# Sturm sweeps of an in-kernel eigensolver: each recurrence step as one double-width product and one sum

## The chip, the cores and the metric

The kernel runs on one core of a Trainium2 chip. The metric is the device time of one execution in microseconds. The kernel before took 2164.6 us (median of three runs, 2164.06 to 2165.33).

## The reference

Four graph layers act one after the other on `x` of 128 graphs with 64 nodes and 256 features in float32; all graphs share one 64x64 matrix `adj`. Each layer is `x = x + layer(relu(layernorm(x)), adj, weights)`.

```
layer 0:  two graph convolutions relu(adj @ (h W + b)), then four small LSTMs
          over windows of 1, 2, 3 and 4 nodes, each writing its last state back
layer 1:  h <- relu(layernorm(L_norm h Wc + bc)) + h with L_norm = 2 adj / lam_max - I
          masked 4-head attention, gelu MLP, layernorms
layer 2:  graph attention (leaky scores, masked softmax)
layer 3:  _, U = eigh(D^-1/2 (deg - adj) D^-1/2)
          out = U relu(U^T h W1 + b1) W2 + ...
```

What matters here is layer 3: it needs all 64 eigenvectors `U` of one 64x64 symmetric matrix. The kernel computes them on the chip itself. The matrix is brought to tridiagonal form with diagonal `D` and off-diagonal `E`. Eigenvalues are then found by multisection: for a trial value x, the number of sign changes in the Sturm sequence

```
p[0] = 1,   p[1] = (d[0] - x) p[0],   p[k+1] = (d[k] - x) p[k] - e[k-1]^2 p[k-1]
```

tells how many eigenvalues lie below x. Every sweep narrows the interval of every eigenvalue to an eighth.

## The kernel before, in words

**Main work.** The 8192 rows of `x` are 64 tiles of 128 rows. Layer 0 works through eight groups of eight tiles: layer norm, two mixing products, the LSTMs, and a transposition back; the results go to DRAM (`put`). The 16 groups of four tiles that follow (the stage called REST in the code, groups from `REST` up) run layers 1, 2 and 3 with their x resident in SBUF, and write the output.

**The eigensolver** (`eig_decomp`, lines 347 to 885, called in line 1107) is a separate group, `EIG` (line 1094), of small instructions on 64 partitions, most of them on VectorE. All its tiles are parts of one large SBUF tile named `arena`, so in a profile everything of it is found under that name until the arena is given to REST. In order of time it does a Householder reduction (62 steps), the set-up of three nested tridiagonal problems (index `l`), nine Sturm sweeps (`NSWEEP`, line 634), a forward and backward quotient recurrence (line 681), eigenvectors, and a correction; lines 1108 to 1113 write the block-diagonal tiles `Ub` and `UTb` that layer 3 needs. The normalising factor for `lapb`, the mixing matrix of layer 1, comes from its own chain of matrix squarings and does not depend on the eigensolver.

**One sweep** (lines 635 to 663). Each of the 64 partitions holds one eigenvalue index. There are C = 21 columns: three problems times KS = 7 trial values. `DX[k]` = d[k] - x is made by six instructions of 448 elements. Then comes the recurrence over k (lines 643 to 653), in which `PL[k]` holds p[k]: a product `DX[k] * PL[k]`, from k = 1 on a product `b = PL[k-1] * E2[k-1]`, and a difference, each 21 elements wide. After every eighth step two neighbouring rows of PL are rescaled by four more instructions. The sweep ends with the signs (`SG`, 1365 elements), the sign changes (`NE`, 1344 elements, written over DX), their count (a reduction over k), a comparison, a sum, and the new lower bounds `lo`, on which the next sweep depends. So the sweeps are one long chain of dependent instructions.

**The order of the work** is neither written by hand nor left to the engines: every instruction is recorded in a `Plan`, which simulates all five engines with a cost for each instruction (lines 176 to 220: for a VectorE instruction on n elements mostly 0.075 + 0.00105 n us, and 0.12 us more until a dependent instruction may begin), and writes the resulting order into each engine's queue. The queues are worked off in that order. `EIG` is the group set aside (line 328): its VectorE and GpSimd instructions have the lowest rank, and are put in only where nothing else is ready; its matmuls have the highest. In the plan, GpSimd and VectorE instructions on SBUF alone also exclude each other. The `arena` counts as a set of spare buffers for REST from the moment at which the last instruction of `EIG` is done (line 963).

Of the kernel before, what the change touches and what calls it, by code (L numbers as in the profile page):

```python
# [8 lines left out]
ALU = mybir.AluOpType  # L9
# [3 lines left out]
N = 64  # L13
KS = 7
# [332 lines left out]
def eig_decomp(plan, room, adj, adjT, ident, idf, ones):  # L347
# [13 lines left out]
    V, G, PE, ACT, SP = (plan.proxy(e) for e in ("V", "G", "PE", "ACT", "SP"))  # L361
# [3 lines left out]
    def scope():  # L365
        inner.reset([0])
        return inner

    def T(shape, name):
        return room.tile(shape)  # L370

    def W(shape, name, bufs=None):

        if bufs is None:
            bufs = 2 if shape[-1] < N or name == "lab" else 1
        ring = kept.setdefault((name, tuple(shape)), [])
        if len(ring) < bufs:
            ring.append(room.tile(shape))
        else:
            ring.append(ring.pop(0))  # L380
        return ring[-1]
# [56 lines left out]
    ph = scope()  # L438
# [4 lines left out]
    for k in range(N - 2):  # L443
# [17 lines left out]
        s = W([N, 1], 's')  # L461
# [21 lines left out]
        p = pf[:N, :2 * N]  # L483
# [43 lines left out]
    M = N - 1  # L527
# [68 lines left out]
    E2 = T([N, 3, N], 'E2')  # L596
# [30 lines left out]
    V.tensor_copy(lo, l1.to_broadcast([N, 3]))  # L627
    C = 3 * KS
    ph = scope()
    PL = ph.tile([N, N + 1, C])  # L630
    V.memset(PL[:, 0, :], 1.0)
    DX = ph.tile([N, N, 3, KS])
    SG = ph.tile([N, N + 1, C])
    for s_ in range(NSWEEP):
        V.tensor_scalar(w, w, 1.0 / (KS + 1), None, op0=ALU.mult)
        x = W([N, 3, KS], 'x')
        V.tensor_scalar(x, c['ramp'], w, None, op0=ALU.mult)
        V.tensor_add(x, x, lo.unsqueeze(2).to_broadcast([N, 3, KS]))
        for l in range(3):
            V.tensor_mul(DX[:, :, l, :], BM[:, l, :].unsqueeze(2).to_broadcast([N, N, KS]), x[:, l, :].unsqueeze(1).to_broadcast([N, N, KS]))  # L640
            V.tensor_sub(DX[:, :, l, :], DM[:, l, :].unsqueeze(2).to_broadcast([N, N, KS]), DX[:, :, l, :])
        DXf = DX.rearrange('p k l s -> p k (l s)')
        for k in range(N):
            V.tensor_mul(PL[:, k + 1, :], DXf[:, k, :], PL[:, k, :])
            if k:
                b = W([N, 3, KS], 'b', 2)
                V.tensor_mul(b, PL[:, k - 1, :].rearrange('p (l s) -> p l s', l=3), E2[:, :, k - 1:k].to_broadcast([N, 3, KS]))
                V.tensor_sub(PL[:, k + 1, :], PL[:, k + 1, :], b.rearrange('p l s -> p (l s)'))
            if k % 8 == 7 and k < N - 1:
                mm = W([N, C], 'mm')  # L650
                V.tensor_reduce(mm, PL[:, k:k + 2, :].rearrange('p k c -> p c k'), op=ALU.max, axis=AX.X, apply_absolute_value=True)
                V.tensor_scalar(mm, mm, 1e-30, None, op0=ALU.max)
                V.reciprocal(mm, mm)
                V.tensor_mul(PL[:, k:k + 2, :], PL[:, k:k + 2, :], mm.unsqueeze(1).to_broadcast([N, 2, C]))
        V.tensor_scalar(SG, PL, 0.0, None, op0=ALU.is_lt)
        NE = DXf
        V.tensor_tensor(NE, SG[:, 1:, :], SG[:, :N, :], op=ALU.not_equal)
        ct = W([N, 3, KS], 'ct')
        V.tensor_reduce(ct.rearrange('p l s -> p (l s)'), NE.rearrange('p k c -> p c k'), op=ALU.add, axis=AX.X)
        V.tensor_tensor(ct, ct, li.unsqueeze(2).to_broadcast([N, 3, KS]), op=ALU.is_le)  # L660
        sm = W([N, 3], 'sm')
        V.reduce_sum(sm, ct, axis=AX.X)
        V.scalar_tensor_tensor(lo, sm, w, lo, op0=ALU.mult, op1=ALU.add)
# [7 lines left out]
    ph = scope()  # L671
# [80 lines left out]
    def one(name):  # L752
        return W([N, 1], name)
# [7 lines left out]
    for l in (1, 0):  # L761
# [10 lines left out]
        b = one('bc')  # L772
# [11 lines left out]
        t = W([N, N], 't64')  # L784
# [3 lines left out]
        t = W([N, N], 't64')  # L788
# [23 lines left out]
        t = W([N, N], 't64')  # L812
# [120 lines left out]
def gnn_kernel(ctx: ExitStack, tc: tile.TileContext, a, out):  # L933
# [171 lines left out]
    room = Carver(arena)  # L1105

    QT, Vc, inner = eig_decomp(plan, room, adj2[:N], adjT2[:N], ident[:N, :N], ident, ones)
    for dst, lhs, rhs in ((Ublk, QT, Vc), (UTblk, Vc, QT)):
        l2 = inner.tile([P, 2, N])
# [564 lines left out]
```

## Time and profile before

| Item | Value |
|---|---|
| median of three runs | 2164.6 us (2164.06 to 2165.33) |
| the profiled execution's own time | 2165.9 us |
| its span, first to last instruction | 2164.1 us |
| outside its span | 1.8 us |
| VectorE busy, instructions | 1800.3 us (83%), 7402 |
| GpSimd busy, instructions | 653.1 us (30%), 968 |
| granted TensorE clock | 0.996 of full speed |

In the profile PE is TensorE's matmuls, PEld its weight loads, DVE is VectorE, ACT ScalarE, POOL GpSimd, SP the DMA-issuing SyncE. Since every instruction is issued by one helper, all have the same line number, L344; groups are told apart by tile and shape. A shape such as 64x21 is partitions times elements. [...]two instructions may overlap in the profile, and a busy VectorE can still take in more work.

### The profile page before, as it was taken

Reading aid. Unit: us, or ns where it says so; the run is one execution under the profiler, and the core shown is the slowest. Engines: PE = TensorE matmul, PEld = TensorE weight load, DVE = VectorE, ACT = ScalarE, POOL = GpSimd, SP = SyncE. Lnnn points to the kernel's source line nnn. Section 1 sums busy time; section 2 is a strip of 40 time slices with the busy share of each in tenths; the row PEclk is TensorE's granted clock in tenths of the full one; section 3 lists DMA queues with packets and bytes.
Section 4 is the critical chain, followed back from the end, with each engine's and each line's share of the span. In section 5 each row is a group of like instructions: output and inputs, shape, how many; then the busy total and the mean of one; then the engine's idle time right before and its main releaser. Section 6 shows DMA issues by size and latency. Waiting matters only on the chain.

```text
span 2164.1 us, 45598 instructions
## 1 busy us (share of the span) xinstructions
PE 2112.6 (98%) x16580; PEld 1630.7 (75%) x16580; DVE 1800.3 (83%) x7402; ACT 1079.8 (50%) x2331; POOL 653.1 (30%) x968
## 2 busy tenths in 40 slices
PE   8999999999999999999999999999999999999997
PEld 6688688688678678678778688766777767776776
DVE  5888788889899999899989887568878868885797
ACT  3354354354354354345345345456566655645673
POOL 7221211210200110110110113654456745554353
PEclk9999999999999999999999999999999999999999
DMA  5000100100100100100000213000010000000001
GB/s 205 2 3 22 41 3 22 40 1 21 40 1 20 40 1 20 40 1 21 26 1 23 69 40 97 21 1 2 21 41 21 21 22 21 12 11 11 1 2 60
DMA packets 44866, 57.67 MB, mean 27 GB/s; under 512 B 8928, under 2 KB 38496, under 8 KB 44640
## 3 DMA queue, kind: packets, MB, share of 16 engines
q1 hardware_dynamic: 43536, 53.71, 7.6%
q8 instruction: 130, 2.13, 0.4%
q10 hardware_dynamic: 1104, 1.05, 0.2%
q14 instruction: 96, 0.79, 0.1%
HBM read 37.53 MB, written 16.78 MB: 25 GB/s over the span
## 4 chain that ended last, share of the span: by engine, by line
PE 83%; DVE 11%; POOL 2%; ACT 1%; DMA 1%; issue 1%; SPq 0%; DVEq 0%; ACTq 0%
PE bank L344 83%; DVE arena L344 3%; DVE big L344 3%; DVE stat L344 2%; DVE mids L344 1%; DVE sums L344 1%; POOL stat L344 1%; POOL sums L344 1%; DMA Wih<-in_WihT_dram 1%; ACT mids L344 0%; ACT arena L344 0%; DMA Whh<-in_L_b_dram 0%; DMA big<-put 0%; ACT big L344 0%; SPq L344 0%
## 5 line engine op out<-in xcount | busy, mean ns | idle before, releaser
L344 PE MATMUL bank<-big,Wih 128*128 128x256 f32 (+3 forms) x2400 | 748.2, 435 | 18.7 <-DVE arena L344 9.3
L344 PEld LDWEIGHTS bank<-big,Wih 128*128 128x128 f32 x2400 | 439.9, 190 | 205.0 <-issue 114.4
L344 ACT ACTIVATE mids<-bank,bl 128x256 f32<-128x256 f32 (+3 forms) x528 | 275.4, 528 | 407.3 <-PE bank L344 403.5
L344 PE MATMUL bank<-big,Whh 128*128 128x256 f32 (+2 forms) x1624 | 431.0, 368 | 3.5 <-DVE big L344 3.5
L344 DVE TENSOR_TENSOR arena<-arena 64x21 f32<-64x21 f32 (+5 forms) x2255 | 372.9, 196 | 35.8 <-POOL arena L344 8.2
L344 PEld LDWEIGHTS bank<-big,Whh 128*128 128x128 f32 x1624 | 294.3, 190 | 42.5 <-issue 10.1
L344 PE MATMUL bank<-big,sums 128*128 128x168 f32 (+2 forms) x1728 | 268.8, 307 | 0.0
L344 PEld LDWEIGHTS bank<-big,sums 128*128 128x128 f32 (+1 forms) x1728 | 225.4, 178 | 16.0 <-issue 3.9
L344 POOL TENSOR_SCALAR stat<-stat 128x4 f32<-128x4 f32 (+1 forms) x228 | 67.9, 299 | 485.4 <-DVE stat L344 472.5
L344 ACT COPY mids<-bank 128x168 f32<-128x168 f32 (+2 forms) x393 | 132.1, 357 | 138.1 <-PE bank L344 135.1
L344 DVE TENSOR_TENSOR big<-mids 128x512 f32<-128x512 f32 (+2 forms) x256 | 142.8, 565 | 31.3 <-ACT mids L344 28.6
L344 ACT ACTIVATE mids<-mids,bl 128x336 f32<-128x336 f32 (+2 forms) x192 | 102.4, 540 | 71.4 <-DVE mids L344 67.6
L344 DVE TENSOR_TENSOR mids<-bank,mids 128x168 f32<-128x168 f32 (+2 forms) x307 | 112.9, 372 | 25.8 <-PE bank L344 22.3
L344 DVE SCALAR_TENSOR_TENSOR arena<-arena 64x1 f32<-64x1 f32 (+15 forms) x565 | 120.9, 237 | 7.5 <-POOL arena L344 3.9
L344 POOL TENSOR_TENSOR big<-big 128x168 f32<-128x168 f32 (+1 forms) x24 | 16.8, 712 | 359.9 <-DVE arena L344 132.2
L344 POOL TENSOR_TENSOR stat<-stat,mhalf 128x4 f32<-128x4 f32 (+1 forms) x114 | 122.1, 1072 | 5.7
L344 ACT ACTIVATE mids<-big 128x256 f32<-128x256 f32 (+2 forms) x176 | 89.4, 509 | 67.7 <-DVE big L344 48.8
L344 PE MATMUL bank<-Wih,big 128*128 128x256 f32 (+1 forms) x512 | 111.7, 358 | 0.2 <-ACT big L344 0.2
L344 DVE TENSOR_SCALAR arena<-arena 64x1 f32<-64x1 f32 (+9 forms) x537 | 104.8, 202 | 8.4 <-POOL arena L344 0.8
L344 DVE TENSOR_TENSOR big<-big,mids 128x256 f32<-128x256 f32 (+2 forms) x200 | 99.3, 498 | 11.1 <-ACT mids L344 10.2
L344 PEld LDWEIGHTS bank<-Wih,big 128*128 128x128 f32 x512 | 87.7, 190 | 15.4 <-issue 4.5
L344 ACT COPY big<-bank 128x512 f32<-128x512 f32 x108 | 59.9, 587 | 55.9 <-PE bank L344 50.8
(357 smaller groups left out, 3568.0 us busy)
## 6 DMA issues: line engine op xcount, KB each, us to landing
big<-in_x_dram SPq DMA_DIRECT2D x30, 512.0 KB, 5.2
put<-big SPq DMA_DIRECT2D x16, 512.0 KB, 3.0
Wih<-in_WihT_dram SPq DMA_DIRECT2D x3, 1024.0 KB, 11.8
Whh<-in_WhhT_dram SPq DMA_DIRECT2D x3, 1024.0 KB, 13.8
big<-put SPq DMA_DIRECT2D x6, 512.0 KB, 5.8
arena<-put SPq DMA_DIRECT2D x6, 512.0 KB, 6.6
out_dram<-big SPq DMA_DIRECT2D x12, 256.0 KB, 2.3
out_dram<-arena SPq DMA_DIRECT2D x12, 256.0 KB, 2.3
```

The source lines that it names most:

```text
L344: getattr(self.engines[op.eng], name)(*map(real, args), **{k: real(a) for k, a in kw.items()})
```

## The change

The two factors of a step lie side by side in one new tile `CO[k]`: columns 0 to 20 hold -e[k-1]^2 (written once, ahead of the sweeps, by three instructions of 441 elements), columns 21 to 41 hold d[k] - x (DX is now a view of this half). One product of 42 elements, `PL[k-1:k+1] * CO[k]`, makes both terms, and one addition of its halves makes `PL[k+1]`. The step k = 0 stays a single product. The signs are written over PL instead of into SG, which goes; therefore row 0 of PL has to be set to 1 again in each sweep, which GpSimd does, where VectorE did it once before. The sign changes are written into the DX half of CO, so that their rows lie 42 elements apart instead of 21, as do those of DX.

```diff
     PL = ph.tile([N, N + 1, C])
-    V.memset(PL[:, 0, :], 1.0)
-    DX = ph.tile([N, N, 3, KS])
-    SG = ph.tile([N, N + 1, C])
+    CO = ph.tile([N, N, 2, C])
+    l3 = lambda t: t.rearrange('p k (l s) -> p k l s', l=3)
+    DX = l3(CO[:, :, 1, :])
+    for l in range(3):
+        V.tensor_scalar(l3(CO[:, 1:, 0, :])[:, :, l, :], E2[:, l, :M].unsqueeze(2).to_broadcast([N, M, KS]), -1.0, None, op0=ALU.mult)
     for s_ in range(NSWEEP):
...
-        DXf = DX.rearrange('p k l s -> p k (l s)')
-        for k in range(N):
-            V.tensor_mul(PL[:, k + 1, :], DXf[:, k, :], PL[:, k, :])
-            if k:
-                b = W([N, 3, KS], 'b', 2)
-                V.tensor_mul(b, PL[:, k - 1, :].rearrange('p (l s) -> p l s', l=3), E2[:, :, k - 1:k].to_broadcast([N, 3, KS]))
-                V.tensor_sub(PL[:, k + 1, :], PL[:, k + 1, :], b.rearrange('p l s -> p (l s)'))
+        G.memset(PL[:, 0, :], 1.0)
+        V.tensor_mul(PL[:, 1, :], CO[:, 0, 1, :], PL[:, 0, :])
+        for k in range(1, N):
+            b = W([N, 2, C], 'b', 2)
+            V.tensor_mul(b, PL[:, k - 1:k + 1, :], CO[:, k])
+            V.tensor_add(PL[:, k + 1, :], b[:, 0, :], b[:, 1, :])
...
-        V.tensor_scalar(SG, PL, 0.0, None, op0=ALU.is_lt)
-        NE = DXf
-        V.tensor_tensor(NE, SG[:, 1:, :], SG[:, :N, :], op=ALU.not_equal)
+        V.tensor_scalar(PL, PL, 0.0, None, op0=ALU.is_lt)
+        NE = CO[:, :, 1, :]
+        V.tensor_tensor(NE, PL[:, 1:, :], PL[:, :N, :], op=ALU.not_equal)
```

## The prediction, made before the changed kernel ran

> **What bounds the kernel now.** I read the busy times first, then a table by stage, then the same table for the tile `arena`, then VectorE in order of time, and last the place where the eigensolver hands over.
>
> ```profile
> PE 2112.6 (98%) x16580; PEld 1630.7 (75%) x16580; DVE 1800.3 (83%) x7402; ACT 1079.8 (50%) x2331; POOL 653.1 (30%) x968
> ```
>
> TensorE is busy for 2112.6 of 2164.1 us and the change leaves its work as it is, so no more than the 51.5 us in which it is idle can be won. The stages show where they lie (columns: window, length, busy PE, PEld, DVE, ACT, POOL):
>
> ```profile
> 598.20:1162.10 563.90, 557.06 (x3271) 441.60 (x3270) 519.30 (x2390) 254.81 (x578) 55.25 (x80) 1.00 0.05 16
> 1162.10:1220.00 57.90, 57.90 (x268) 48.49 (x268) 51.61 (x254) 23.54 (x52) 0.00 (x0) 1.00 0.08 24
> 1220.00:1338.00 118.00, 109.32 (x543) 89.92 (x543) 98.00 (x432) 52.14 (x121) 21.12 (x34) 0.99 0.29 93
> 1338.00:1362.00 24.00, 24.00 (x114) 21.13 (x113) 14.08 (x49) 16.68 (x37) 20.25 (x26) 1.00 0.00 1
> 1362.00:2164.00 802.00, 777.65 (x8564) 576.72 (x8563) 621.83 (x1703) 464.59 (x807) 412.56 (x553) 1.00 0.06 18
> ```
>
> The first window holds eight of the nine sweeps: TensorE is idle for 563.90 - 557.06 = 6.8 us in it. In the third the eigensolver's rest runs beside the last group of layer 0, and 8.7 us are idle. REST has 24.4 us. The sweeps thus lie under a full TensorE. For the `arena` alone, the window of the sweeps reads:
>
> ```profile
> 598.20:1162.10 563.90, 0.00 (x0) 0.00 (x0) 339.66 (x1863) 0.00 (x0) 0.00 (x0) 1.00 0.05 16
> ```
>
> So 2390 - 1863 = 527 VectorE instructions of layer 0 are strewn among 1863 of the sweeps. The sign-change instructions (1344 elements) mark the first and the ninth sweep:
>
> ```profile
> 598.16 1.55 DVE L344 TENSOR_TENSOR arena<-arena 64x1344 f32<-64x1344 f32 x1
> ```
>
> ```profile
> 1162.11 1.54 DVE L344 TENSOR_TENSOR arena<-arena 64x1344 f32<-64x1344 f32 x1
> ```
>
> That is 563.95 / 8 = 70.5 us a sweep. VectorE in order of time (start, length, engine, operation, count) shows what a step is made of:
>
> ```profile
> 655.02 0.26 DVE L344 TENSOR_TENSOR arena<-arena 64x21 f32<-64x21 f32 x2
> ...
> 656.54 0.38 DVE L344 TENSOR_TENSOR arena<-arena 64x21 f32<-64x21 f32 x2
> ...
> 658.45 1.61 DVE L344 TENSOR_TENSOR arena<-arena 64x21 f32<-64x21 f32 x11
> ...
> 663.27 0.40 DVE L344 TENSOR_TENSOR arena<-arena 64x42 f32<-64x42 f32 x2
> ```
>
> One such instruction lasts some 0.17 us. Two in 0.26 us start 0.09 apart: the second does not need the first. Two in 0.38 us start 0.21 apart: a dependent pair (the last steps ahead of a rescaling). Eleven in 1.61 us are ten distances in 1.44, or 0.43 for three. So a step of three is no sum of three durations: it is two dependent passages, product to difference and difference to next product, 2 x 0.21 = 0.42 us, and `b`, which needs nothing new, lies in the shadow of the first. The 42-wide rescaling product and its 21-wide successor start 0.40 - 0.17 = 0.23 apart.
>
> [...]177 and 197:
>
> ```profile
> L344 DVE TENSOR_TENSOR arena<-arena 64x21 f32<-64x21 f32 x1728 | 239.8, 177 | 16.1
> ...
> L344 DVE TENSOR_TENSOR arena<-arena 64x42 f32<-64x42 f32 x63 | 12.4, 197 | 1.7
> ```
>
> Doubling the width costs 0.02 us. [...]removing the instruction in the shadow does not shorten a chain. [...]
>
> **The change part by part.**
>
> *The steps.* Nine sweeps x 63 steps = 567. Removed: 567 instructions, all from the shadow. Left are two dependent passages, 0.23 from the wide product to the sum and 0.21 from the sum to the next product: 0.44 us against 0.42, so 567 x 0.02 = 11 us more if nothing comes between. What is won is room: of a step's 0.42 us, three starts of about 0.09 to 0.10 take 0.29 and 0.13 stand empty; afterwards 0.09 + 0.11 = 0.20 of 0.44 are taken and 0.24 stand empty, in two gaps. Layer 0's instructions may lie in those gaps. How well do they today? A sweep alone is 63 x 0.42 = 26.5, seven rescalings of about 1.0 (0.19 + 0.17 + 0.28 + 0.20 with waits), six products and differences of 0.64 less 0.03 overlap = 3.7, signs 0.8, changes 1.5, count 3.1, small ones 1: 43.6 us. 563.9 - 8 x 43.6 = 215 us for 527 instructions, 0.41 each; their busy time is (519.30 - 339.66) / 527 = 0.34. So the gaps are hardly used. With 527 x 9/8 = 593 in all sweeps, the new gap of 0.11 could save at most 62 us (567 x 0.11), at least nothing. Many come in rows, of which only the first finds a gap, and one that arrives late in a gap pushes the chain: I take 10 us. Net of both: +1 us.
>
> *Count of the changes.* 9 x 3.07 us at twice the distance: [...]at worst twice as long, +27.6. I take 0. Signs in place and strided writes in runs of 7 or 21: 0, the same element counts.
>
> *New once:* three instructions of 441 elements, between 0.3 (as fast as the signs per element) and 0.64 (the 448-wide product): 1.7 us. VectorE's single memset goes: -0.1.
>
> *GpSimd's memset,* nine times: it waits for the sign changes of the sweep before and the first product waits for it. Between lie the count (3.07), the comparison, the bounds and six 448-wide instructions (3.7), over 7 us, while GpSimd is busy for 55 of 564 us. If that cover failed, all of VectorE's queue, layer 0 included, would stand behind that product, and TensorE's banks behind it. 0 taken; it is bounded by 9 x 0.5, half the row of a 128x512 memset pair of 1.00 us. No DMA is added or moved.
>
> *Sum:* the eigensolver ends +1 + 1.7 - 0.1 = about 3 us later, bounds -60 (62 saved, 2 added) and +45 (11 + 2 + 27.6 + 4.5). What does that move? The last write of the eigensolver, the first use of an arena buffer by REST on ScalarE as it ends, and TensorE's first read of one:
>
> ```profile
> 1337.87 0.23 DVE L344 COPY UTb<-bank 64x64 f32<-64x64 f32 x1
> ```
>
> ```profile
> 1343.96 1.58 ACT L344 ACTIVATE arena<-big,stat 128x256 f32<-128x256 f32 x3
> ```
>
> ```profile
> 1365.63 3.71 PE L344 MATMUL bank<-lapb,arena 64*64 64x64 f32 x236
> ```
>
> ScalarE has filled them at 1345.5; TensorE works at layer 0 until 1362 and reads them at 1365.6. So an earlier end wins nothing there, and a later one is covered for 20 us. Three microseconds move nothing: **no change**, 2164.6 by the median. The profiled execution took 2165.9 = 2164.1 span + 1.8 around it, 1.3 above the median, and I apply the difference of nothing to the median; I say 2164.0 since more free slots on VectorE can only help layer 0's own instructions a little.
>
> The costs in the plan follow the same picture (0.097 + 0.11 for a 21-wide passage), so it will write an order with nearly the same end of the eigensolver. But every choice from the first sweep on can fall otherwise, and in REST 24.4 us of stalls hang on such choices: a scatter of a few us either way that no row lets me compute.
>
> **The rivals.**
> *Faster, the room is used.* If layer 0's instructions fill the gaps, the sweeps end up to 60 us earlier, the rest of the eigensolver moves from the last group of layer 0 to where TensorE is full anyway, and the 8.7 us of stalls of that stage mostly go: 2164 - 7 = 2157. For it: 527 instructions find 0.24 us per step. Against it: they fill little today.
> *Slower, the end comes too late.* The strided count doubles (+27.6) and the gaps stay empty (+11 + 2): 41 us. Beyond 20 us TensorE meets REST buffers that are not filled. 41 - 20 = 21 us, half of them covered by blocks in other buffers: +10, 2174. It decides from a delay of 20 us.[...]
> *The change doesn't do what it says* cannot be: the counts follow from the loop.
>
> **How the numbers follow.** About 0.2%, 4.3 us, is what can be told from no change here. No change 0.38 (2160.3 to 2168.9 as its own range, 2164.0 predicted), faster 0.34, slower 0.28; the scatter of the order gives the two sides more than their mechanisms would alone. Range 2153 to 2175: from the faster case with 4 us of scatter to the slower one with 1.
>
> **What would show it.** 64x21 products and sums 1728 - 1134 = 594, 64x42 ones 63 + 567 = 630, VectorE 7402 - 565 = 6837 instructions, GpSimd 977. Two dependent instructions in a step at 0.23 and 0.21: if nearer than that, my chain is wrong. Sweeps 70 us apart: at 65 or less the room is used. The count at 3.07 us. `UTb` written at 1341: before 1310 or after 1358 one of the rivals holds. It would be wrong altogether if TensorE's stalls in the sweeps (6.8 us) changed by more than 3.

## The result, and the profile after

| | Before | After |
|---|---|---|
| median, runs side by side | 2164.76 us (2163.33 to 2165.35, 6 runs) | 2172.11 us (2170.70 to 2174.17, 6 runs) |
| profiled execution, its span | 2165.9 us, 2164.1 us | 2172.2 us, 2170.4 us |
| mean granted TensorE clock in it | 0.996 | 0.992 |

The ratio is 1.0030, with a 95% interval of 1.0020 to 1.0041. The change makes the kernel slower by 0.3%, 7.3 us.

Busy time and instructions of each engine, of the changed kernel:

```profile
PE 2120.1 (98%) x16580; PEld 1635.6 (75%) x16580; DVE 1765.8 (81%) x6837; ACT 1075.4 (50%) x2329; POOL 656.1 (30%) x977
```

VectorE has 565 instructions fewer and GpSimd 9 more, as foretold. But look at TensorE. It executes the same 16580 matmuls and is busy for 7.5 us longer (2112.6 before), while its idle time has hardly changed: 2170.4 - 2120.1 = 50.3 us against 51.5. So in this execution the loss is not time in which TensorE waits; the same work takes longer.

The table by stage of the changed kernel, with the same windows as before (window, length, busy PE, PEld, DVE, ACT, POOL, then the granted clock):

```profile
598.20:1162.10 563.90, 556.95 (x3274) 442.04 (x3273) 499.70 (x1890) 254.24 (x581) 57.37 (x88) 0.99 0.06 18
1162.10:1220.00 57.90, 57.90 (x264) 48.02 (x263) 51.60 (x244) 22.63 (x51) 0.00 (x0) 1.00 0.04 15
1220.00:1338.00 118.00, 109.38 (x540) 89.54 (x539) 97.43 (x444) 52.67 (x125) 19.86 (x34) 0.99 0.27 76
1338.00:1362.00 24.00, 24.00 (x113) 21.12 (x112) 12.44 (x47) 16.24 (x37) 21.11 (x26) 1.00 0.16 59
1362.00:2164.00 802.00, 781.21 (x8562) 579.14 (x8561) 610.83 (x1701) 461.92 (x806) 414.16 (x553) 0.99 0.05 17
```

TensorE is idle for 6.95 us in the window of the sweeps (6.84 before) and for 8.6 in the third (8.7 before). One pair of matmuls, which every kernel here executes once, marks on TensorE where REST begins. The tables by tile give its first and last start, before and after:

```profile
L344 PE MATMUL bank<-UTb,ones x2: 272/274/275, 1362.7 to 1362.8; 128*128 128x128 f32 x2
```

```profile
L344 PE MATMUL bank<-UTb,ones x2: 273/274/275, 1363.3 to 1363.4; 128*128 128x128 f32 x2
```

Up to there only 0.6 us is lost. From there to the end of the span it takes 2164.1 - 1362.7 = 801.4 us before and 2170.4 - 1363.3 = 807.1 after. So nearly the whole loss, 5.7 us of 6.3, arises in REST, where no instruction was changed; TensorE is even busier in the window after 1362, 781.21 us of 802 against 777.65.

The eigensolver's last write and a row of seven instructions of the recurrence, VectorE of the changed kernel in order of time:

```profile
643.26 1.50 DVE L344 TENSOR_TENSOR arena<-arena 64x42 f32<-64x42 f32 x7
```

```profile
1336.92 0.23 DVE L344 COPY UTb<-bank 64x64 f32<-64x64 f32 x1
```

Seven instructions in 1.50 us, the last one of 0.17, make six distances in 1.33: 0.222 each, 0.44 for a step of two. `UTb` is written at 1336.92, 1 us earlier than before.

Where does TensorE become slower? A stretch of REST in the changed kernel, TensorE in order of time (start, length, engine, operation, count, and in brackets the idle time ahead of it and who ended it):

```profile
1677.14 3.62 PE L344 MATMUL bank<-Wih,big 128*128 128x256 f32 x16
...
1683.06 2.05 PE L344 MATMUL bank<-Wih,mids 128*128 128x128 f32 x16 [0.58 <-ACT mids L344]
1687.61 0.69 PE L344 MATMUL bank<-UTb,Whh 64*64 64x64 f32 x32 [2.50 <-DVE Whh L344]
1688.23 1.12 PE L344 MATMUL bank<-ident,big 128*128 128x128 f32 x7
1690.64 3.78 PE L344 MATMUL bank<-Wih,big 128*128 128x256 f32 x8 [1.29 <-DVE big L344]
```

At 1677, 16 matmuls of 128x256 take 3.62 us. At 1690, after waits of 0.58, 2.50 and 1.29 us, 8 of the same kind take 3.78: half the speed. The same 50 us in the changed kernel and in the one before:

```profile
1650.00:1700.00 50.00, 45.62 (x563) 37.09 (x563) 44.97 (x142) 25.81 (x48) 29.18 (x47) 0.93 0.14 44
```

```profile
1650.00:1700.00 50.00, 49.14 (x582) 38.44 (x581) 46.34 (x132) 28.54 (x50) 31.56 (x40) 1.00 0.15 44
```

The clock was 0.93 against 1.00, and 4.4 us were idle against 0.9. In the trace's record of the granted clock the stretches at half speed sum to 20.2 us before (6.8 at the start, then 3.4 at 897, 3.4 at 1238, 3.4 at 2125 and 3.1 at the end) and to 36.3 after (10.2 at the start, 6.8 at 894, 3.4 at 1238, 6.8 at 1689, 3.4 at 2129, 3.4 at 2163 and 2.2 at the end). 16.1 us more at half speed are 8 us lost, about the 7.5 us by which TensorE is busier. 9.3 of the 16.1 us, 4.7 us lost, lie in REST (6.8 at 1689, and 9.0 against 6.5 near the end).

This execution overstates the clock's part somewhat: its mean granted clock of 0.992 is the lowest of the six runs of the changed kernel, whose mean is 0.9937. The three sets of runs of the kernel before that stand beside the experiments have 0.9959 to 0.9965 on average. At half speed half of the time is lost, so the loss is 1 minus the clock, times the span: 13.7 us against 7.5 to 8.8. By this estimate 5 to 6 of the 7.3 us are the clock's.

What lies ahead of the 6.8 us at half speed? They begin at 1689.0, behind the waits of 0.58 and 2.50 us and ahead of the one of 1.29; in the 3.41 us before, half as long as the stretch itself, TensorE was still busy for 1.34 us (window, length, busy PE, PEld, DVE, ACT, POOL, clock):

```profile
1685.54:1688.95 3.41, 1.34 (x39) 1.28 (x39) 3.41 (x17) 2.08 (x4) 3.07 (x6) 1.00 0.00 0
```

### The profile page after: what moved, and what is told of

The parts are those of the page before. It is cut to its first block, busy times and chain, and to the rows that moved or that the text cites. A ratio compares the mean times of both kernels' runs of the same rounds, so it can differ in the third digit from the quotient of the medians.

```text
span 2170.4 us, 45040 instructions
## 1 busy us (share of the span) xinstructions
PE 2120.1 (98%) x16580; PEld 1635.6 (75%) x16580; DVE 1765.8 (81%) x6837; ACT 1075.4 (50%) x2329; POOL 656.1 (30%) x977
## 4 chain that ended last, share of the span: by engine, by line
PE 88%; DVE 7%; POOL 2%; issue 1%; ACT 1%; DMA 0%; SPq 0%; DVEq 0%; ACTq 0%; POOLq 0%
PE bank L344 88%; DVE big L344 3%; DVE stat L344 2%; DVE arena L344 2%; POOL stat L344 1%; DVE mids L344 1%; POOL big L344 0%; ACT arena L344 0%; POOL arena L344 0%; ACT mids L344 0%; DMA big<-put 0%; DVE sums L344 0%; ACT sums L344 0%; ACT big L344 0%; DMA adj<-in_adj_dram 0%
## 5 line engine op out<-in xcount | busy, mean ns | idle before, releaser
L344 PE MATMUL bank<-big,Wih 128*128 128x256 f32 (+3 forms) x2368 | 733.0, 434 | 15.9 <-DVE big L344 8.0
L344 PE MATMUL bank<-big,Whh 128*128 128x256 f32 (+2 forms) x1608 | 423.4, 365 | 3.6 <-DVE big L344 3.6
L344 DVE TENSOR_TENSOR arena<-arena 64x42 f32<-64x42 f32 (+6 forms) x1686 | 347.7, 207 | 51.1 <-POOL arena L344 8.9
L344 POOL TENSOR_SCALAR stat<-stat 128x4 f32<-128x4 f32 (+1 forms) x228 | 74.5, 328 | 375.1 <-DVE stat L344 362.2
L344 POOL MEMSET arena<- 64x2 f32 (+6 forms) x81 | 8.6, 111 | 438.1 <-DVE arena L344 438.1
L344 ACT ACTIVATE mids<-big 128x512 f32<-128x512 f32 (+2 forms) x176 | 89.6, 510 | 73.9 <-DVE big L344 60.8
L344 DVE TENSOR_TENSOR mids<-bank,mids 128x168 f32<-128x168 f32 (+2 forms) x292 | 103.1, 357 | 16.8 <-PE bank L344 13.6
L344 PE MATMUL bank<-Wih,big 128*128 128x256 f32 (+1 forms) x376 | 87.3, 374 | 1.8 <-DVE big L344 1.8
L344 POOL TENSOR_TENSOR arena<-arena 64x1 f32<-64x1 f32 x66 | 43.7, 662 | 146.2 <-ACT arena L344 103.3
L344 DVE BATCH_NORM_STATS2 stat<-big 128x6 f32<-128x256 f32 x232 | 85.2, 406 | 2.7 <-DMA big<-put 2.6
## 6 DMA issues: line engine op xcount, KB each, us to landing
Whh<-in_WhhT_dram SPq DMA_DIRECT2D x3, 1024.0 KB, 13.7
```

Of the source, the lines that this page charges most:

```text
L344: getattr(self.engines[op.eng], name)(*map(real, args), **{k: real(a) for k, a in kw.items()})
```

## The experiments

Theory O (order): the new instructions cost and win nothing; but the planner lays out anew all work that follows, and the order that it happens to find for REST is worse than the one before, through waits of TensorE and the half clock after them. Theory I (instructions): the new instructions themselves cost the time, by their width, by GpSimd's part in the chain, or by the strided rows.

### The new instructions in the old order

```diff
-                for name, args, kw in op.calls:
+                for eng, name, args, kw in op.instead() if op.instead else [(op.eng, *c) for c in op.calls]:
...
             V.tensor_mul(PL[:, k + 1, :], DXf[:, k, :], PL[:, k, :])
...
+                b2 = W([N, 2, C], 'b2', 2)
+                wide = [('V', 'tensor_mul', (b2, PL[:, k - 1:k + 1, :], CO[:, k]), {})]
...
+                instead(('V', 'tensor_add', (PL[:, k + 1, :], b2[:, 0, :], b2[:, 1, :]), {}))
```

> The changed instructions (wide product, sum, signs in place, memset on GpSimd, three factor writes) stand in the places that the plan of the kernel before gave to the old ones; every other instruction on every engine keeps the order of before. If the slowdown comes from the order that the plan wrote: within 2 us of before, 2163 to 2167. If it comes from the instructions themselves (longer chain, memset, strides): 2170 to 2174, as the changed kernel. If the new steps win something that the new order hides: below 2162.

Measured: 2168.12 us (13 runs) against 2166.00 of the kernel before beside it; ratio 1.0007, interval 0.9998 to 1.0015. `UTb` is written at 1337.02. The time is 1 us above the 2167 that theory O allowed, but the kernel before beside it is 1.2 us higher than in the result, too; the ratio is what counts. The new instructions, put where the old ones stood, can't be told from no change: they cost at most 0.15%, 3 us, and the change costs at least 0.20%. So theory I falls as the cause of the whole loss, and with it every term of the prediction's sum.

### The old instructions in the new order

```diff
...
+            instead(('V', 'tensor_mul', (PL[:, k + 1, :], DYf[:, k, :], PL[:, k, :]), {}), ('V', 'tensor_mul', (b1, r3(PL[:, k - 1, :]), E2[:, :, k - 1:k].to_broadcast([N, 3, KS])), {}))
...
+            instead(('V', 'tensor_sub', (PL[:, k + 1, :], PL[:, k + 1, :], b1.rearrange('p l s -> p (l s)')), {}))
...
```

> The reverse: the old three instructions a step, the separate sign tile and one memset on VectorE, in the places of the order that the plan wrote for the changed kernel. Order theory: 2170 to 2174, slow with the old instructions. Instruction theory: 2163 to 2167.

Measured: 2193.27 us (4 runs), ratio 1.0129, 1.0113 to 1.0144: 21 us over the changed kernel, with the same order on TensorE. Both theories missed that. Here is the window of the sweeps of this kernel:

```profile
598.20:1162.10 563.90, 548.46 (x3158) 423.39 (x3157) 514.92 (x2302) 244.43 (x552) 56.28 (x80) 0.99 0.05 16
```

TensorE is idle for 15.4 us instead of 6.95, and `UTb` is written at 1359.36. So the new order does use room that the shorter steps leave; with the third instruction back in it, VectorE comes late for layer 0 (from 560 to 1220 us TensorE waits 8.1 us for VectorE's `big`, and 4.9 in the changed kernel). The room of the prediction exists and the new order counts on it, but TensorE had nothing to win there.

The pair that marks the beginning of REST starts at 1385.7 in this kernel, 23 us later than in the kernel before, so this loss lies ahead of REST. From the pair to the end of the span it takes 805.5 us: near the 807.1 of the changed kernel, where the old order has 801.4 (kernel before) and 800.6 (new steps in the old order). In these profiles, one of each kernel, REST is thus 4 to 6 us longer in the new order, with either kind of step.

### Only one instruction of three in each step, old order

```diff
...
                 V.tensor_mul(b, PL[:, k - 1, :].rearrange('p (l s) -> p l s', l=3), E2[:, :, k - 1:k].to_broadcast([N, 3, KS]))
+                plan.ops[-1].instead = lambda: []
                 V.tensor_sub(PL[:, k + 1, :], PL[:, k + 1, :], b.rearrange('p l s -> p (l s)'))
+                plan.ops[-1].instead = lambda: []
```

> In the order of before, each step of the recurrence keeps only its first product; the second product and the difference are left out (the recurrence is not computed), so 1134 VectorE instructions and one of the two dependent passages are gone. If the sweeps are hidden under TensorE: the eigensolver ends no earlier in the order, VectorE idles instead, and the time falls by no more than the 8.7 us of stalls in the last group of layer 0, likely by 0 to 4 us (2160 to 2165). If VectorE's load in the sweeps limits layer 0: faster by more than 10 us.

Measured: 2166.71 us (13 runs), ratio 1.0004, 0.9996 to 1.0012. The busy times of this kernel:

```profile
PE 2113.5 (98%) x16580; PEld 1631.5 (75%) x16580; DVE 1683.2 (78%) x6268; ACT 1079.3 (50%) x2331; POOL 650.4 (30%) x968
```

With 1134 instructions and 117 us of busy VectorE gone, the time stays and `UTb` is written at 1336.28 instead of 1337.87. This also corrects how a sweep is to be read: in a given order its 70 us are not the length of its chain; it advances at the pace of layer 0's instructions between which it is strewn, and those at TensorE's pace.

### Only the memset moved

```diff
-    V.memset(PL[:, 0, :], 1.0)
+    G.memset(PL[:, 0, :], 1.0)
```

> The kernel before with one edit: the single memset of row 0 of PL is done by GpSimd instead of VectorE, once. No instruction of a sweep changes. If the plan's order is a matter of chance that any small edit throws anew: the time moves by more than 0.1% (2 us) either way, as far as the whole change does (about 7 us). If the slowdown needs the new steps: 2164 to 2166.

Measured: 2176.19 us (5 runs), ratio 1.0046, 1.0034 to 1.0059. One instruction of 0.1 us, executed once, moved from one engine to another, costs as much as the whole change (the intervals overlap). No duration of an instruction explains that; what is left is the order. The clock record of this kernel has, among others, 10.2 us at half speed at 731, 6.8 at 1694 and 8.1 at the end. Not all of its loss lies in REST, which begins at 1366.6, 4 us later than before.

### The memsets back on VectorE

```diff
-        G.memset(PL[:, 0, :], 1.0)
+        V.memset(PL[:, 0, :], 1.0)
```

> The changed kernel, with its memset of row 0 of PL issued on VectorE in every sweep instead of on GpSimd; everything else is the same, and the order is planned anew. Theory 'order' (the new instructions cost nothing, the plan throws the order of all later work anew and the new order of REST happens to be some 6 us worse): the nine memsets weigh nothing (9 x 0.1 us in a queue with room), the order of TensorE's queue differs in thousands of places once more, and the time is another draw, anywhere in 2160 to 2182. Rival 'GpSimd' (the memset on another engine is what costs, by its wait between two engines in each sweep): about 2165, the end of the eigensolver 5 us earlier than in the changed kernel. A time near 2165 would thus fit both; the end of the eigensolver tells them apart.

Measured: 2174.13 us (5 runs), ratio 1.0042, 1.0029 to 1.0054. `UTb` is written at 1337.62, no earlier than with GpSimd (1336.92). The rival expected 2165. GpSimd's part in the chain is not the cause; this is one more order.

### Another order of REST, no instruction changed

```diff
-            return 0.4 if op.group >= REST and op.group != EIG else 0.12
+            return 0.42 if op.group >= REST and op.group != EIG else 0.12
```

> The kernel before with not one instruction changed: only the plan's allowance ahead of TensorE's instructions in REST is 0.42 us instead of 0.40, so that near ties in REST fall otherwise. The order of layer 0 and of the eigensolver stays as it was up to about 1430 us. Theory 'order': the time moves by several us although no work is changed, to either side: 2158 to 2180, more likely up than down if 2165 is a good draw. Rival 'instructions' (orders of REST are worth the same, and the 7 us of the change come from its instructions): 2165 within 2 us.

> The changed kernel with the same allowance of 0.42 us. Its order stays as it was up to about 1655 us, just ahead of the stretch in which TensorE stalls for 4.4 us and then works at half its clock for 6.8 us. Theory 'order': the time moves by several us from 2172, to either side, with all that the change touches left alone; if this one stretch is what is lost and the new order has none like it, 2165. Rival 'instructions': 2172 within 2 us.

Measured: the kernel before with this edit 2171.09 us (6 runs), ratio 1.0028, 1.0017 to 1.0040; the changed kernel with it 2169.99 us (7 runs), 1.0022, 1.0011 to 1.0033. The first is the clearest of all: no instruction is changed, only which of nearly equal choices in REST the planner takes, and 5.3 us (2171.09 - 2165.82, the kernel before beside it) are lost. Its clock is 0.996, as before; so the half clock is one way in which an order costs, not the only one. The second can't be told from the changed kernel (1.0020 to 1.0041), so it decides nothing between the two theories. It doesn't escape the stall: its clock is 0.93 from 1650 to 1700, too.

### The stall filled with matmuls

```diff
+FILL = {10945: 9, 10948: 4}
...
+                for i in range(FILL.get(op.index, 0) if op.eng == "PE" else 0):
+                    self.engines["PE"].matmul(op.calls[0][1][0].val.pool[op.calls[0][1][0].val.buf][:, :P], self.fill, self.fill, start=True, stop=True)
...
+    plan.fill = ones
```

The first of two runs had 20 and 10 in place of 9 and 4.

> The changed kernel in its own order, with 30 matmuls of 128x128 whose results are overwritten: 20 of them[...] put into TensorE's queue where it waits for 2.50 us at 1685, and 10 where it waits for 1.29 us at 1689. They fill waits and make nothing ready earlier. Theory 'half clock follows the stall': the stretch of 6.8 us at half the clock from 1689 on is gone or shorter, and the time is 3.4 us less, near 2169; the waits themselves remain lost. Rival 'the half clock has another cause'[...]: the stretch stays, 2172 or 1 us more. Rival 'the stall alone counts': no change either.

> The changed kernel in its own order with 9 and 4 filling matmuls in the two waits instead of 20 and 10. In the first filling each took 4.63 / 20 = 0.23 us, twice what was reckoned, so that the filling outlasted the waits by 4.63 + 2.40 - 3.79 = 3.2 us, about what the full clock gave back; 9 and 4 last 2.1 and 0.9 us and end within the waits. Theory 'half clock follows the stall': no stretch at half the clock at 1689, and 3.4 us less than the changed kernel: 2168 to 2169.5. Rival 'nothing is won' (what TensorE does sooner it waits for later): no stretch at half the clock, yet 2172.

Measured: with 20 and 10, 2173.07 us (5 runs), ratio 1.0038, 1.0024 to 1.0052. With 9 and 4, 2168.27 us (13 runs), ratio 1.0009, 1.0001 to 1.0018, where the changed kernel has 1.0020 to 1.0041. TensorE in order of time, first with 20 and 10, then with 9 and 4:

```profile
1691.60 4.63 PE L342 MATMUL bank<-ones 128*128 128x128 f32 x40
...
1697.61 2.40 PE L342 MATMUL bank<-ones 128*128 128x128 f32 x20
1699.84 1.89 PE L344 MATMUL bank<-Wih,big 128*128 128x256 f32 x8
```

```profile
1685.39 2.17 PE L342 MATMUL bank<-ones 128*128 128x128 f32 x18
1688.04 0.69 PE L344 MATMUL bank<-UTb,Whh 64*64 64x64 f32 x32 [0.48 <-DVE Whh L344]
1688.67 0.98 PE L344 MATMUL bank<-ident,big 128*128 128x128 f32 x7
1689.49 1.06 PE L342 MATMUL bank<-ones 128*128 128x128 f32 x8
1691.08 1.99 PE L344 MATMUL bank<-Wih,big 128*128 128x256 f32 x8 [0.53 <-DVE big L344]
```

In both the eight matmuls behind the stall take 1.9 to 2.0 us instead of 3.78: the half clock follows the idle time and goes with it. The profiles of the other kernels agree. The changed kernel, the old steps in the new order, the moved memset, the memsets on VectorE and the changed kernel with 0.42 all have this wait of some 2.5 us ahead of `bank<-UTb,Whh`, and all five have a stretch of 3.4 or 6.8 us at half speed behind it; the two filled ones have none.

In the first the filling outlasted the waits, and its time can't be told from the changed kernel's. In the second it fits, and work that computes nothing makes the kernel faster: by 3.8 us (2172.11 - 2168.27), or 4.5 us by the ratios (1.0030 - 1.0009), where the lost clock let 3.4 be expected. The two medians are from different sets of runs, so the ratios count; their intervals are disjoint, though only just (1.0018 and 1.0020). The mean granted clock of the 13 runs is 0.9955, which is 9.7 us lost instead of the changed kernel's 13.7.

### A later end of the eigensolver

The prediction held that a later end is covered for 20 us. To see it, 57 in-place instructions were put ahead of the last matmul of the eigensolver, first into the finished order, then recorded ahead of the planning.

```diff
         V.tensor_copy(l2, lhs.unsqueeze(1).to_broadcast([P, 2, N]))
+        plan.ops[-1].calls += [('tensor_scalar', (l2[:, :, :1], l2[:, :, :1], 1.0, None), dict(op0=ALU.mult))] * (57 if dst is UTblk else 0)
```

```diff
         V.tensor_copy(l2, lhs.unsqueeze(1).to_broadcast([P, 2, N]))
+        for _ in range(57 if dst is UTblk else 0):
+            V.tensor_scalar(l2[:, :, :1], l2[:, :, :1], 1.0, None, op0=ALU.mult)
```

> The kernel before in its own order, with 57 dependent in-place instructions of two elements a partition (about 0.2 us each, some 10 to 12 us together) put into VectorE's queue just ahead of the eigensolver's last matmul, so that UTb is written that much later, at some 1349. The theory of the prediction (a later end is covered for 20 us, since TensorE reads REST's buffers only at 1365.6): no change, 2165 to 2167. Rival 'the queue itself' (the last matmul of the eigensolver has its fixed place in TensorE's queue, and what stands behind it there waits too, as do layer 0's VectorE instructions behind the 57): 2172 to 2177, nearly the whole delay.

> The same 57 instructions, but recorded one by one before the planning, so that the plan knows of them and places the eigensolver's last matmul and layer 0's instructions around them; the order of REST is then another one as well. If the cover of 20 us is real and only the fixed order of the one above breaks it: 2165 plus the scatter of a new order of REST, 2165 to 2177, with TensorE's stalls from 1220 to 1363 as before (about 9 us). If there is no cover: 2175 to 2185, with 10 us more of stalls in that stage.

Measured: in the finished order 2181.80 us (5 runs), ratio 1.0067, 1.0055 to 1.0080. Planned, 2174.87 us (5 runs), ratio 1.0041, 1.0028 to 1.0053. In the finished order, TensorE and VectorE in order of time:

```profile
1333.47 11.56 DVE L344 TENSOR_SCALAR arena<-arena 128x2 f32<-128x2 f32 x57
```

```profile
1345.18 0.66 PE L344 MATMUL bank<-arena 128*128 128x64 f32 x2 [11.30 <-DVE arena L344]
```

TensorE stands at the eigensolver's own matmul, which has its place in the queue, for 11.3 us with layer 0's ready work behind it, and the clock record has 13.7 us at half speed from 1337.5 on. The time is above even what the rival expected (2172 to 2177). In the planned one the matmul stands later in the queue. The 20 us from 1330 on, there:

```profile
1330.00:1350.00 20.00, 19.79 (x97) 16.84 (x97) 14.90 (x80) 6.14 (x14) 0.00 (x0) 1.00 0.00 1
```

`UTb` is written at 1350.2 and TensorE doesn't wait. So, for a delay of 12 us, the cover exists if the planner knows of it and not in the fixed order. The planned one's 8 us over the kernel before lie in REST, which begins at 1362.2 as before, with half-clock stretches at 1386, 1645 and at the end: a new order again.

### The kernel before, filled

```diff
+FILL = {14476: 5, 14479: 4}
...
```

The other lines are those of the filling above.

> The kernel before in its own order with 5 and 4 filling matmuls (0.23 us each) where TensorE waits for 1.46 us at 2122 and 1.21 us at 2124.6, ahead of its stretch of 3.4 us at half the clock. Theory 'half clock follows the stall': that stretch is gone and the time is 1.7 us less than before, 0.1%, at the edge of what five rounds tell. Rival 'another cause': the stretch stays.

Measured: 2164.67 us (21 runs) against 2166.53 (33 runs) beside it; ratio 0.9992, 0.9986 to 0.9999. This is the fastest of the kernels here, by 1.9 us, though only just outside what can be told from none; it keeps the old steps and beats both kernels.

The stretch at 2125 is gone from the clock record. That alone doesn't show that the filling removed it: those at 897 and 1238 are gone as well, and nobody filled those waits. Here are the same two waits unfilled, first in the kernel before, then with the new steps in the old order, which has the same order of REST:

```profile
2123.46 1.16 PE L344 MATMUL bank<-sums,big 64*64 64x64 f32 x64 [1.46 <-ACT sums L344]
2125.83 3.48 PE L344 MATMUL bank<-Whh,big 128*128 128x256 f32 x8 [1.21 <-ACT big L344]
```

```profile
2122.52 1.16 PE L344 MATMUL bank<-sums,big 64*64 64x64 f32 x64 [1.46 <-ACT sums L344]
2124.89 1.99 PE L344 MATMUL bank<-Whh,big 128*128 128x256 f32 x8 [1.22 <-ACT big L344]
```

In the second the eight matmuls run at the full clock. What differs is where the waits fall. In the clock record the stretches at half speed lie on a grid of 3.41 us, whose place differs from execution to execution (the first stretch begins at 9.20 us in the kernel before, at 9.59 in the changed one). In the kernel before, one window of the grid, just ahead of the stretch, holds most of both waits; in the other execution they are shared by two windows:

```profile
2122.05:2125.46 3.41, 1.16 (x64) 1.02 (x64) 3.35 (x18) 2.11 (x5) 0.66 (x1) 1.00 0.00 0
```

```profile
2120.37:2123.79 3.42, 1.85 (x71) 1.52 (x69) 3.36 (x18) 2.12 (x6) 0.16 (x1) 1.00 0.00 0
2123.79:2127.20 3.41, 2.16 (x9) 1.61 (x10) 3.41 (x13) 1.15 (x3) 2.36 (x5) 1.00 0.24 76
```

TensorE was busy for 1.16 of 3.41 us there, and for 1.85 and 2.16 here. So this stretch is a matter of chance from one execution to the next. The mean of 21 runs speaks for the filling: 0.9971 of the full clock against 0.9965 for the 33 beside it, an estimated 1.4 of the 1.9 us.

## Why the prediction was wrong

*Right, and shown.* The counts; the step of two at 0.44 us (0.444); sweeps 70 us apart (1165.53 - 600.99 = 564.5 over eight, 70.6); the end of the eigensolver nearly unmoved (1336.9 for a foretold 1341, 1337.9 before); TensorE's stalls in the sweeps unmoved (6.95 for 6.84); no cost of GpSimd's memset that could be seen (2172.1 with it, 2174.1 with the memsets on VectorE). The core of the argument, that the sweeps lie under a full TensorE and that their instructions move nothing, is shown by the new steps in the old order (1.0007) and by the sweeps with two thirds of their step removed (1.0004).

*Mis-sized, or right for another reason.* The count of the sign changes became shorter, 2.64 us for 3.07. It did so wherever its rows lay 168 bytes apart, in either order (2.63 with the new steps in the old order; 3.08 with the old steps in the new one); that it would cost no more at that distance was my estimate, which no trace of the kernel before shows, and nothing hung on it. The three factor writes took 1.1 us for a foretold 1.7. The plan's allowance for a dependent VectorE instruction is 0.12 us, not the 0.11 of the prediction. The 20 us of cover are not there in a fixed order, as shown above; the change never needed them. The sum of +3 us took the 70 us of a sweep for its chain and what lies between its links; the sweeps with two thirds of their step removed show that TensorE sets their pace, so that the end came out so near is no support for the sum. And the 51.5 us of idle time are not all that could be won: part of the busy time runs at half speed, by the profile's clock of 0.996 (9 us of 2164.1) a loss too.

*The step that failed* is the last one: the new order of all later work was put at nothing on average, "a scatter of a few us either way that no row lets me compute", and "no change" was concluded from the three microseconds alone. Those three microseconds do move nothing, as the new steps in the old order show. I named the re-drawn order but centred its scatter on the kernel before, and I priced it by TensorE's stalls alone: TensorE's 2112.6 us of busy time I took as fixed, since its work stays. With the same 16580 matmuls they became 2120.1, through the clock.

For six kernels the planner drew the order of REST anew: this change 2172.1, the moved memset 2176.2, the memsets on VectorE 2174.1, the other allowance 2171.1 and 2170.0, the planned delay 2174.9. All six are slower than the kernel before, by 0.2 to 0.5%; the two in which only instructions changed and the order stayed (1.0007 and 1.0004) can't be told from it. The simplest reading is that the order before was a good draw, and that each of the edits of the eigensolver tried here gave it up for an ordinary one, whatever the edit itself was worth. It is a reading: were the seven orders equal draws, the one before would be the best of them in one case of seven. With the six known, the forecast would have been 2165 + 4 to 10.

The measured 2172.1 lies within the range of 2153 to 2175 that was stated. That is luck: its upper end was built on an eigensolver that ends too late, and it ended 1 us earlier.

The mechanism of more than half of the loss is shown: the stall at 1685 and the half clock behind it, since filling it took the ratio from 1.0030 to 1.0009, about 4.5 of 6.5 us; the intervals leave room for anything from a little to nearly all. Some 2 us, why the new order has this stall, and what makes one order better than another apart from the clock, as with the other allowance on the kernel before, stay open.

## What to carry to other kernels

Where a greedy planner writes the order, a small edit has two effects: its own, and a new draw of everything behind it; test the first by issuing the new instructions in the old places before believing either. If the order at hand is a good draw, as it seems to be here, the second effect is a loss on average, and should be priced as one. On a TensorE-bound kernel compare TensorE's busy time, not only its idle time: here a busy time that grew with the same instructions (2112.6 to 2120.1 us) was the clock, and filling the waits ahead of it with matmuls whose results are thrown away won a part of it back (ratio 1.0030 to 1.0009). One profile is not enough for such stretches, since they came and went here from one execution to the next, as the one at 2125 did; compare the granted clock over many runs.

## What the runs showed of the hardware

- Half the clock followed waits shorter than one window of 3.41 us: one of 2.50 us (changed kernel, half speed from 1689.0 on), or 1.46 and 1.21 us close together (kernel before, from 2125.5 on), the latter not in every execution.
- Where the waits lay on the clock's grid of 3.41 us mattered. In the profiles of the two kernels, after their first 40 us, eight windows at full clock were followed by half speed. TensorE was busy for 0.27, 0.34 and 0.36 of them in the kernel before (from 1234.6, 2122.1 and 893.3 us on) and for 0.24, 0.30, 0.39, 0.43 and 0.52 in the changed one (890.2, 1235.0, 1685.5, 2125.9, 2160.0). The other 1225 were followed by full speed; the least busy of them have 0.42, 0.50 and 0.53. TensorE's busy time is modelled in the profile, so these shares are estimates.
- A float32 matmul instruction of 128x128 in the code is two in the profile: 20 filled 4.63 us as 40, 0.23 us for each of the 20 (run with 20 and 10).
- A reduction over k of 64 x 21 x 64 float32 took 2.64 us with its elements 168 bytes apart and 3.07 with 84; no run shows why. VectorE of the new steps in the old order and of the kernel before:

```profile
601.15 2.63 DVE L344 TENSOR_REDUCE arena<-arena 64x21 f32<-64x1344 f32 x1
```

```profile
600.24 3.08 DVE L344 TENSOR_REDUCE arena<-arena 64x21 f32<-64x1344 f32 x1
```
